# Four normalised residual layers on one core: the norms' inverse roots computed by Newton steps on GpSimd, and the sigmoid table loaded once

## The chip, the cores and the metric

The kernel runs on one core of a Trainium2 chip. The metric is the device time of one execution in microseconds (us), as the median of several runs. The engines of the core are called PE (TensorE, the matrix engine), DVE (VectorE), ACT (ScalarE) and POOL (GpSimd); SP (SyncE) issues most of the DMAs. Each engine carries out its own instructions in the order in which the program lists them, and waits for the others through semaphores.

## The reference

The input x has the shape 4 x 32 x 32 x 16. Four layers run one after the other, each as `x = x + L(_gn(x))`. The norm `_gn` forms, for each image and each group of two channels, the mean and the variance over all pixels of the group:

```python
m = jnp.mean(g, axis=(1, 2, 4), keepdims=True)
s = jnp.var(g, axis=(1, 2, 4), keepdims=True)
return ((g - m) / jnp.sqrt(s + eps)).reshape(v.shape)     # eps = 1e-5
```

Layers 0, 1 and 3 are convolutions whose 3x3 filters G differ at each of the 1024 output positions: `first` is a product of the positions with a 1024 x 1024 matrix M, and `second` is the sum over all pixels of W times `relu(input - shifted)`, where `shifted` is the image filtered with that position's filters. Layer 2 is an interval layer: running maxima and minima over a triangle, two steps of `max(sigmoid(ft + rt + b))`, and a last sigmoid.

## The kernel before, in words

The images are handled as two groups g of two. The three convolutions on two groups make six phases (`phases`, L90); a phase has 8 chunks of 128 output positions, a chunk 32 steps, so 256 steps a phase and 1536 in all. A step (L719) is one filter channel f of one image b. Each step lists, in this order:

- one resumption of the generator `prep_parts` (L220), which gets the filters of later steps ready;
- `first_part` of this step (L644): 8 matmuls into a pair of PSUM banks and an ACT pass over them (L665);
- `second_part` of the step before (L668): 6 more matmuls into its banks, and then one DVE instruction, called junk here (L682), which takes the minimum with zero, multiplies by W and sums. The pool of bank pairs has four buffers (L80), so the first product of a step needs that the junk four steps earlier is done;
- where its pause has run out, one resumption of the generator `behind` (L735), which carries everything else: norms, interval layer, the next phase's images, the products with M.

The engines are not in step with one another; a step only says where in each engine's list an instruction stands.

`prep_parts` gets one unit of filters (4 channels, used in 8 steps) ready in 8 resumptions, two units ahead of its use. With k for the resumption, 0 to 7: k=0 `upper` on DVE (L203, tile upper_w), which needs that POOL has centred this unit's raw filters; k=1 an ACT pass (L175); k=2 an ACT pass and on POOL the tensor operations of L237 and L238; k=3 an ACT pass and on POOL L241 and four casts (L243, L245); k=4 on POOL the centring of the raw filters of the NEXT unit (L214, tile raw); k=6 on SP two copies of the parts and the load of later raw filters (L251, L110). In phase 0 the resumptions begin at step 3 with two extra ones at steps 20 and 24, so that from step 24 on, and in every later phase, step s of a phase has k = (s - 1) mod 8. The tile upper_w has two buffers, parts has three.

`behind` says by the value that it yields how many steps it pauses. The value IDLE (0) means: go on at the next step whose resumption of `prep_parts` allows it (k = 0, 4, 5, 6, 7). So each pause in `behind` sets which k its next piece of work falls on, and what stands ahead of it on POOL, DVE, ACT and SP.

`group_norm` (L315) occurs eight times: c00 and c10 in phase 0, c01 in phase 1, c11 in phase 2, i0 and c02 in phase 3, i1 and c12 in phase 4 (the letter says convolution or interval layer, then for c the group and the convolution, for i the group). DVE reduces (`sums`, `totals`, L317 to L341), POOL centres and squares (L347 to L351), DVE reduces again and ends with the transpose `whole`; then ACT takes the root (L361), DVE the reciprocal (L363), and POOL multiplies (L364). Between `sums` of the squares and its `totals` stands a one-element Sqrt (L356), to have the table of Sqrt loaded in time, and in `step` of the interval layer a one-element Sigmoid (L593) ahead of the real one (L596). ACT has one set of tables active at a time; the compiler puts an ACT_TABLE_LOAD ahead of an activation whose function is not in it. The first Sqrt of the kernel is that of the opening (L834), which stays.

After i0 and i1, DVE transposes the normalised images in two pieces (L510), at two neighbouring steps. `split` and `difference` (L274, L286) put two more kinds of POOL operations (L280, L288) into the end of the work for a next phase, and `place` (L290) twelve DMAs for each image. `first_terms` (L420) multiplies both groups with M, 128 small matmuls in a row (L427).

Of the kernel before, what the change touches and what calls it, by code (L numbers as in the profile page):

```python
# [8 lines left out]
F32 = mybir.dt.float32  # L9
F32R = mybir.dt.float32r  # L10
I32 = mybir.dt.int32
AF = mybir.ActivationFunctionType
ALU = mybir.AluOpType
AX = mybir.AxisListType

P = 128
# [3 lines left out]
GC = GB * C  # L20
NL = 3
NP = H * H
# [22 lines left out]
def net_kernel(ctx: ExitStack, tc: tile.TileContext, x, xq, xi, convs, iv_w, iv_b, out):  # L45
# [26 lines left out]
    nc = tc.nc  # L72
# [4 lines left out]
    work = ctx.enter_context(tc.tile_pool(name="work", bufs=1))  # L77
# [5 lines left out]
    def bank_pair(name):  # L83
        return psum.tile([P, 2, 512], F32, tag="ps", name=name)
# [13 lines left out]
    IDLE = 0  # L98
# [55 lines left out]
    spare = const.tile([1, 1], F32, name="spare")  # L154
    nc.gpsimd.memset(spare, 0.0)
    eps = const.tile([P, 1], F32, name="eps")
# [152 lines left out]
    def spread(stat):  # L309
        return stat.unsqueeze(1).unsqueeze(3).to_broadcast([P, NT, GC // 2, 2])  # L310

    def pair_view(ap):
        return ap.rearrange("p t (g s) -> p t g s", s=2)

    def group_norm(g, name, dst, gap):  # L315


        def sums(src):
            nc.vector.tensor_reduce(
                part[:, : GC // 2], src.rearrange("p t (g s) -> p g t s", s=2), axis=AX.XY, op=ALU.add  # L320
            )

        def totals(name):

            turned = work.tile([P, 32], F32, tag="turned", name=f"turned_{name}")
            nc.vector.transpose(turned, part)
            by_quarter = work.tile([32, 4], F32, tag="by_quarter", name=f"by_quarter_{name}")
            for q in range(4):
                nc.vector.tensor_reduce(
                    by_quarter[:, q : q + 1], turned[32 * q : 32 * q + 32], axis=AX.X, op=ALU.add  # L330
                )
            yield gap
            total = work.tile([P, 32], F32, tag="total", name=f"total_{name}")
            for q in range(4):
                nc.vector.tensor_reduce(
                    total[32 * q : 32 * q + 32, 0:1], by_quarter, axis=AX.X, op=ALU.add
                )
            yield gap
            whole = work.tile([P, 32], F32, tag="whole", name=f"whole_{name}")
            nc.vector.transpose(whole, total[:, 0:1].to_broadcast([P, 32]))  # L340
            return whole[:, : GC // 2]  # L341

        sums(X[g])
        yield gap
        m = yield from totals(f"m{name}")
        mean = work.tile([P, GC // 2], F32, tag="mean", name=f"mean_{name}")
        nc.gpsimd.tensor_scalar_mul(mean, m, 1.0 / (2 * NP))  # L347
        xc = work.tile([P, NT, GC], F32, tag="xc", name=f"xc_{name}")
        nc.gpsimd.tensor_tensor(pair_view(xc), pair_view(X[g]), spread(mean), ALU.subtract)
        sq = work.tile([P, NT, GC], F32, tag="sq", name=f"sq_{name}")  # L350
        nc.gpsimd.tensor_tensor(sq, xc, xc, ALU.mult)  # L351
        yield 4
        sums(sq)
        yield gap
        yield IDLE
        nc.scalar.activation(spare, spare, AF.Sqrt)  # L356
        v = yield from totals(f"v{name}")
        yield 2
        yield IDLE
        rstd = work.tile([P, GC // 2], F32, tag="rstd", name=f"rstd_{name}")  # L360
        nc.scalar.activation(rstd, v, AF.Sqrt, bias=eps, scale=1.0 / (2 * NP))  # L361
        yield 2
        nc.vector.reciprocal(rstd, rstd)  # L363
        nc.gpsimd.tensor_tensor(pair_view(dst), pair_view(xc), spread(rstd), ALU.mult)  # L364
        yield 3

# [4 lines left out]
    def before_conv(g, layer):  # L371
        xn = work.tile([P, NT, GC], F32, tag="xn", bufs=2, name=f"xn_{g}_{layer}")
        xns[g] = xn
        yield from group_norm(g, f"c{g}{layer}", xn, 1 if layer == 2 else 4)


# [43 lines left out]
    def first_terms(layer, mt):  # L420


        sums = bank_pair(f"pf_{layer}")
        for g in range(NG):
            for pt in range(NT):
                for j in range(4):
                    nc.tensor.matmul(  # L427
                        sums[32 * j : 32 * j + 32, g, :256],
                        lhsT=xns[g][:, pt, :], rhs=mt[:, pt, j, :],
                        start=pt == 0, stop=pt == NT - 1, tile_position=(0, 32 * j),  # L430
                    )
        ft = work.tile([P, NG, NT * GC], F32, tag="fs", name=f"ft_{layer}")
        for g in range(NG):
            nc.vector.transpose(ft[:, g], sums[:, g, : NT * GC])
        yield 1
        for g in range(NG):
            nc.vector.tensor_tensor(
                X[g], X[g], ft[:, g].rearrange("p (t m) -> p t m", t=NT), ALU.add
            )
            yield 1  # L440
# [45 lines left out]
    def interval_layer(g):  # L486
# [4 lines left out]
        n = H * H  # L491
# [10 lines left out]
        nc.gpsimd.memset(r[:R, :, 0:1], 0.0)  # L502
        nc.gpsimd.memset(r[:R, H:], 0.0)
        yield from group_norm(g, f"i{g}", xi, 2)

        raw = one[:GC].rearrange("p (j t r) -> p r t j", j=H, r=ROWS)
# [65 lines left out]
        def step(name, ftp, bias):  # L572

            ft = ivp.tile([P, QI, T1], F32, tag="ft", name=f"ft_{name}{g}")
            nc.scalar.copy(ft, ftp)
            yield 2
            s = ivp.tile([P, QI, T1], F32, tag="s", name=f"s_{name}{g}")
            last = None
            for i in range(QI + 1):
                if i < QI:  # L580
                    t = dp[i % 2]
                    nc.gpsimd.tensor_tensor(
                        t,
                        ft[:, i, :].unsqueeze(1).to_broadcast([P, T1, T1]),
                        rt,
                        ALU.add,
                    )
                if last is not None:
                    nc.vector.tensor_reduce(s[:, i - 1, :], last, axis=AX.X, op=ALU.max)
                last = t  # L590
                yield 6 if i < QI else 3
            yield IDLE
            nc.scalar.activation(spare, spare, AF.Sigmoid)  # L593
            yield 2
            yield IDLE
            nc.scalar.activation(s, s, AF.Sigmoid, bias=bias)  # L596
            for q in range(NQ):
                nc.sync.dma_start(r[R:, QI * q : QI * (q + 1), :], s[GC * q : GC * (q + 1)])
            yield 4

        yield from right_side("r0", iv["r0"])
        ftp = left("l0", iv["f0"])
        yield from step("a", ftp, bv[:, 0:1])
        yield from right_side("r1", iv["r1"])
        ftp = left("l1", iv["f1"])
        yield from step("b", ftp, bv[:, 1:2])
        z = left("l2", iv["f2"])
        y = ivp.tile([P, QI, H], F32, tag="y", name=f"y_{g}")
        nc.scalar.activation(y, z[:, :, 1:], AF.Sigmoid, bias=bv[:, 2:3])
        yield 2  # L610
        y = y.rearrange("p i j -> p (i j)")
# [370 lines left out]
```

## Time and profile before

| | |
|---|---|
| three runs | 2480.47, 2481.87, 2485.29 us; median 2481.87 |
| the profiled execution, its own time | 2481.97 us |
| its span in the profile | 2480.3 us, granted clock 1.00 |
| PE busy | 2458.5 us, 99% |
| DVE busy | 2086.0 us, 84% |
| ACT busy | 1878.2 us, 76% |
| POOL busy | 1579.3 us, 64% |
| PE idle for ACT / for DVE's junk / for a parts DMA | 5.2 / 2.9 / 1.7 us in all |
| table loads | 5: one for L834, two for L356, two for L593, 1.283 us each |

A busy share is an average over the whole span. The PE row says how little can be won, because the other engines' time lies beside PE's. Which engine holds PE up, and where, is read from the view of waits and from the timeline of a stretch, where each line has the start, the length, the engine, the line of the code and the tiles.

### The profile page before, as it was taken

The page shows a single profiled execution, that of the slowest core. Times are in us where ns is not written, and L with a number is a line of the kernel's source. Part 1 is how long each engine was busy: PE and PEld are TensorE (multiplying, and loading weights), DVE is VectorE, ACT ScalarE, POOL GpSimd, SP SyncE. Part 2 cuts the span into 40 slices and gives each one's busy share as a digit, 9 for nine tenths or more (in the row PEclk, how much of TensorE's full clock was granted, in tenths as well). Part 3 has the DMA queues.
Part 4 walks back from the last instruction along what each step waited for, and adds up shares of the span by engine and source line. Part 5 has one row for each costly group of instructions (what it writes and reads, how often), then busy time and mean ns, then how long its engine had stood idle before and what let it go on. Part 6 is the DMA issues. An engine that isn't in the chain of part 4 may idle for free.

```text
span 2480.3 us, 58060 instructions
## 1 busy us (share of the span) xinstructions
PE 2458.5 (99%) x21906; PEld 2074.2 (84%) x21906; DVE 2086.0 (84%) x3617; ACT 1878.2 (76%) x2181; POOL 1579.3 (64%) x1750
## 2 busy tenths in 40 slices
PE   8999999999999999999999999999999999999999
PEld 4888888888888888888888989888989888888887
DVE  8888878888888888788898988899889888788887
ACT  3778767787777778677777777787777787677776
POOL 4766655667555667555567777586778676555552
PEclk9999999999999999999999999999999999999999
DMA  6556744465454457544454545574455477554442
GB/s 189 140 144 183 213 131 134 138 180 157 137 145 137 137 157 193 176 137 137 137 145 119 143 126 139 146 195 124 129 139 145 120 187 201 150 145 137 137 137 54
DMA packets 97673, 366.92 MB, mean 148 GB/s; under 512 B 26480, under 2 KB 31472, under 8 KB 97392
## 3 DMA queue, kind: packets, MB, share of 16 engines
q1 hardware_dynamic: 95696, 361.57, 52.9%
q8 instruction: 172, 2.82, 0.5%
q10 hardware_dynamic: 1568, 1.62, 0.3%
q14 instruction: 109, 0.89, 0.1%
q0 software_dynamic: 128, 0.02, 0.0%
HBM read 199.78 MB, written 1.02 MB: 81 GB/s over the span
## 4 chain that ended last, share of the span: by engine, by line
PE 94%; DVE 2%; DMA 2%; issue 1%; ACT 1%; POOL 0%; SPq 0%; ACTq 0%; DVEq 0%; POOLq 0%
PE pc L629 92%; DVE junk L682 1%; PE pf L427 1%; DMA parts<-parts 1%; ACT pc L665 0%; DMA raw<-in_xi 0%; DMA raw<-in_g 0%; DMA ia<-first 0%; PE ps_l L550 0%; DMA first<-in_g 0%; PE ps_r L563 0%; DVE tables L510 0%; DVE raw L848 0%; DVE upper_w L203 0%; SPq L302 0%
## 5 line engine op out<-in xcount | busy, mean ns | idle before, releaser
L682 DVE SCALAR_TENSOR_TENSOR junk<-pc,WT 128x1024 f32<-128x1024 f32 x1536 | 1880.0, 1224 | 363.6 <-PE pc L629 316.8
L665 ACT ACTIVATE pc<-pc 128x1024 f32<-128x1024 f32 x1520 | 1531.8, 1008 | 556.1 <-PE pc L629 531.6
L629 PE MATMUL pc<-ib,parts 64*128 64x512 f32 x6080 | 953.0, 387 | 4.7 <-DVE junk L682 2.9
L629 PE MATMUL pc<-iyz,parts 64*128 64x512 f32 x6080 | 950.3, 387 | 5.3 <-ACT pc L665 5.2
L629 PE MATMUL pc<-ia,parts 64*128 64x496 f32 x6080 | 928.5, 379 | 0.0
L629 PEld LDWEIGHTS pc<-ib,parts 64*128 64x128 f32 x6080 | 585.1, 184 | 109.3 <-DVE junk L682 8.5
L629 PEld LDWEIGHTS pc<-ia,parts 64*128 64x128 f32 x6080 | 587.6, 184 | 106.2
L629 PEld LDWEIGHTS pc<-iyz,parts 64*128 64x128 f32 x6080 | 586.2, 184 | 94.9 <-ACT pc L665 9.4
L629 PE MATMUL pc<-im,W 64*128 64x496 f32 x3072 | 606.4, 384 | 0.0
L237 POOL TENSOR_TENSOR parts<-raw,upper_w 128x512 fp32r<-128x512 f32 x190 | 249.0, 1311 | 496.3 <-DVE upper_w L203 447.3
L629 PEld LDWEIGHTS pc<-im,W 64*128 64x128 f32 x3072 | 297.8, 184 | 57.3 <-issue 3.6
L243 POOL CAST parts<-parts 32x512 fp32r<-32x512 f32 x380 | 231.2, 608 | 48.8 <-ACT parts L240 30.5
L238 POOL TENSOR_TENSOR W<-W,raw 128x512 fp32r<-128x512 f32 x190 | 246.9, 1300 | 7.8 <-ACT W L175 7.8
L241 POOL TENSOR_TENSOR parts<-parts 128x512 fp32r<-128x512 f32 x190 | 246.5, 1297 | 2.2 <-ACT parts L236 2.0
L245 POOL CAST parts<-upper_w 32x512 fp32r<-32x512 f32 x380 | 231.6, 609 | 22.8
L214 POOL TENSOR_TENSOR raw<-raw,ident 128x512 f32<-128x512 f32 x190 | 199.5, 1050 | 61.5 <-DMA raw<-in_g 36.6
L175 ACT ACTIVATE W<-raw,low_w 128x512 fp32r<-128x512 f32 x190 | 136.2, 717 | 9.2 <-DMA ia<-first 9.2
L682 DVE DVE_READ_ACCUMULATOR junk<-pc,WT 128x1 f32 x1536 | 127.8, 83 | 0.0
L236 ACT ACTIVATE parts<-upper_w 128x512 fp32r<-128x512 f32 x190 | 118.8, 625 | 4.8 <-DVE upper_w L203 4.7
L240 ACT CAST parts<-upper_w 128x512 fp32r<-128x512 f32 x190 | 116.6, 614 | 0.0
L697 POOL TENSOR_SCALAR acc<-acc 128x32 f32<-128x32 f32 x40 | 16.7, 417 | 136.5 <-DVE junk L682 134.6
L203 DVE TENSOR_SCALAR upper_w<-raw 128x512 int32<-128x512 int32 x190 | 85.2, 449 | 2.7 <-POOL raw L214 2.3
(139 smaller groups left out, 479.1 us busy)
## 6 DMA issues: line engine op xcount, KB each, us to landing
raw<-in_g SPq DMA_DIRECT2D x190, 768.0 KB, 7.1
parts<-parts SPq DMA_DIRECT2D x380, 384.0 KB, 5.0
WT<-in_w SPq DMA_DIRECT2D x48, 512.0 KB, 4.6
MT<-in_mt SPq DMA_DIRECT2D x24, 512.0 KB, 7.9
raw<-xs SPq DMA_DIRECT2D x120, 71.8 KB, 3.1
ib<-temp SPq DMA_DIRECT2D x40, 128.0 KB, 2.4
ia<-temp SPq DMA_DIRECT2D x80, 62.0 KB, 3.4
raw<-in_xi SPq DMA_DIRECT2D x3, 287.0 KB, 5.0
```

The costliest lines, as they stand in the source:

```text
L175: nc.scalar.activation(dst, src, AF.Copy, scale=mask[:, 1:2])
L214: eng.tensor_tensor(raws[u][:, s, at:to], raws[u][:, s, at:to], pick[s][:, f0 + at : f0 + to].unsqueeze(2).to_broadcast([P, to - at, P]), ...
L236: nc.scalar.activation(WD, high, AF.Copy, scale=-EPS)
L237: nc.gpsimd.tensor_tensor(WL, w8, high, ALU.subtract)
L238: nc.gpsimd.tensor_tensor(W9, W9.bitcast(F32), src[:, 2], ALU.add)
L240: nc.scalar.copy(WU, high)
L241: nc.gpsimd.tensor_tensor(WD, WD.bitcast(F32), WL.bitcast(F32), ALU.add)
L243: nc.gpsimd.tensor_copy(WU[hi], WL[lo].bitcast(F32))
L245: nc.gpsimd.tensor_copy(WL[lo], high[hi])
L629: nc.tensor.matmul(ps[:, h, at : at + n], lhsT=w[r], rhs=v[r] if n == NH else v[r][:, :n], start=first and k == 0, stop=k == len(pairs) - ...
L665: nc.scalar.activation(ps, ps, AF.Copy, scale=1.0 + EPS)
L682: nc.vector.scalar_tensor_tensor(junk, ps.rearrange("p h n -> p (h n)"), 0.0, chunks[n], op0=ALU.min, op1=ALU.mult, accum_out=accs[phase][ ...
```

## The change

A new generator `inverse_root` replaces the ACT root and the DVE reciprocal of a norm. POOL forms a = v/2048 + 1e-5; DVE forms a first guess y of the inverse root from a's bits with two integer operations (a shift, then a subtraction from a constant); POOL halves and negates a, and then makes four Newton steps of four operations each, y = y (1.5 + a y y), with a pause of one step behind each. All are on tiles of 128 x 16 elements. The one-element Sqrt ahead of it is taken out, and with it two IDLE pauses and two of two steps; a pause of one step comes in. In the interval layer, the one-element Sigmoid of `step` goes, with an IDLE pause and one of two steps. One one-element Sigmoid is put into `first_terms`, for the first convolution only, behind its matmuls in the program.

```diff
--- before.py
+++ after.py
@@ -312,6 +312,28 @@
     def pair_view(ap):
         return ap.rearrange("p t (g s) -> p t g s", s=2)
 
+    def inverse_root(v, name):
+
+        n = GC // 2
+        a, y, t = (
+            work.tile([P, n], F32, tag=tag, name=f"{tag}_{name}") for tag in ("root_a", "root_y", "root_t")
+        )
+        nc.gpsimd.tensor_scalar(a, v, 1.0 / (2 * NP), 1e-5, op0=ALU.mult, op1=ALU.add)
+        nc.vector.tensor_scalar(
+            t.bitcast(I32), a.bitcast(I32), 1, None, op0=ALU.logical_shift_right
+        )
+        nc.vector.tensor_scalar(
+            y.bitcast(I32), t.bitcast(I32), -1.0, float(0x5F3759DF), op0=ALU.mult, op1=ALU.add
+        )
+        nc.gpsimd.tensor_scalar_mul(a, a, -0.5)
+        for _ in range(4):
+            nc.gpsimd.tensor_tensor(t, a, y, ALU.mult)
+            nc.gpsimd.tensor_tensor(t, t, y, ALU.mult)
+            nc.gpsimd.tensor_scalar(t, t, 1.5, None, op0=ALU.add)
+            nc.gpsimd.tensor_tensor(y, y, t, ALU.mult)
+            yield 1
+        return y
+
     def group_norm(g, name, dst, gap):
 
 
@@ -352,15 +374,9 @@
         yield 4
         sums(sq)
         yield gap
-        yield IDLE
-        nc.scalar.activation(spare, spare, AF.Sqrt)
         v = yield from totals(f"v{name}")
-        yield 2
-        yield IDLE
-        rstd = work.tile([P, GC // 2], F32, tag="rstd", name=f"rstd_{name}")
-        nc.scalar.activation(rstd, v, AF.Sqrt, bias=eps, scale=1.0 / (2 * NP))
-        yield 2
-        nc.vector.reciprocal(rstd, rstd)
+        yield 1
+        rstd = yield from inverse_root(v, name)
         nc.gpsimd.tensor_tensor(pair_view(dst), pair_view(xc), spread(rstd), ALU.mult)
         yield 3
 
@@ -429,6 +445,8 @@
                         lhsT=xns[g][:, pt, :], rhs=mt[:, pt, j, :],
                         start=pt == 0, stop=pt == NT - 1, tile_position=(0, 32 * j),
                     )
+        if layer == 0:
+            nc.scalar.activation(spare, spare, AF.Sigmoid)
         ft = work.tile([P, NG, NT * GC], F32, tag="fs", name=f"ft_{layer}")
         for g in range(NG):
             nc.vector.transpose(ft[:, g], sums[:, g, : NT * GC])
@@ -589,9 +607,6 @@
                     nc.vector.tensor_reduce(s[:, i - 1, :], last, axis=AX.X, op=ALU.max)
                 last = t
                 yield 6 if i < QI else 3
-            yield IDLE
-            nc.scalar.activation(spare, spare, AF.Sigmoid)
-            yield 2
             yield IDLE
             nc.scalar.activation(s, s, AF.Sigmoid, bias=bias)
             for q in range(NQ):
```

## The prediction, made before the changed kernel was run

> **What bounds the kernel now.** I read the page first, then PE's waits, then the timelines around a table load and around the norm i0. The page says that PE is full:
>
> ```profile
> PE 2458.5 (99%) x21906; PEld 2074.2 (84%) x21906; DVE 2086.0 (84%) x3617; ACT 1878.2 (76%) x2181; POOL 1579.3 (64%) x1750
> ```
>
> No PE work is added or removed, so the change can only alter the 21.8 us in which PE is idle (2480.3 - 2458.5). PE's waits, with total, number and longest:
>
> ```profile
> PE pc L629 <- ACT pc L665: 5.2, 7, 1.6
> ...
> PE pc L629 <- DVE junk L682: 2.9, 8, 0.8
> ```
>
> Of the 5.2 us on ACT, 3.2 us lie before 60 us and 0.4 us at the very end; the four others are one gap of 0.38 to 0.39 us at each of the four table loads of L593 and L356. The first of these on ACT (start, length):
>
> ```profile
> 1423.04 1.01 ACT L665 ACTIVATE pc<-pc 128x1024 f32<-128x1024 f32 x1 [0.56 <-PE pc L629]
> 1424.06 1.28 ACT L593 ACT_TABLE_LOAD   x1
> 1425.36 0.20 ACT L593 ACTIVATE spare<-spare 1x1 f32<-1x1 f32 x1
> 1425.47 1.89 ACT L665 ACTIVATE pc<-pc 128x1024 f32<-128x1024 f32 x2
> ```
>
> ACT idles 0.56 us per step, and a step lasts 1.567 us (the pitch of the waiting junks): most of the load is absorbed. Now POOL and DVE around i0:
>
> ```profile
> 1273.91 1.30 POOL L237 TENSOR_TENSOR parts<-raw,upper_w 128x512 fp32r<-128x512 f32 x1 [5.46 <-DVE upper_w L203]
> 1275.16 1.30 POOL L238 TENSOR_TENSOR W<-W,raw 128x512 fp32r<-128x512 f32 x1
> 1276.41 1.31 POOL L241 TENSOR_TENSOR parts<-parts 128x512 fp32r<-128x512 f32 x1
> 1277.79 1.27 POOL L243 CAST parts<-parts 32x512 fp32r<-32x512 f32 x2
> 1279.12 1.27 POOL L245 CAST parts<-upper_w 32x512 fp32r<-32x512 f32 x2
> 1280.48 1.04 POOL L214 TENSOR_TENSOR raw<-raw,ident 128x512 f32<-128x512 f32 x1
> ```
>
> ```profile
> 1284.83 0.42 DVE L203 TENSOR_SCALAR upper_w<-raw 128x512 int32<-128x512 int32 x1
> ...
> 1287.96 1.31 DVE L510 STREAM_TRANSPOSE tables<-xi 32x256 f32<-32x256 f32 x2
> 1289.31 1.23 DVE L682 SCALAR_TENSOR_TENSOR junk<-pc,WT 128x1024 f32<-128x1024 f32 x1
> ...
> 1290.57 1.30 DVE L510 STREAM_TRANSPOSE tables<-xi 32x256 f32<-32x256 f32 x2
> 1291.90 1.23 DVE L682 SCALAR_TENSOR_TENSOR junk<-pc,WT 128x1024 f32<-128x1024 f32 x1
> ```
>
> The reader is to see a loop: `upper` on DVE starts POOL's unit, and POOL's last operation of the unit (L214, done at 1281.52) is what the next `upper` reads. That one comes at 1284.83, so POOL has 3.3 us in hand, once a unit. DVE's own slack follows from the two transposes: the junk at 1291.90 is 1.95 us behind the pitch, and PE waited 0.21 us there, so DVE may fall some 1.74 us behind before PE stops.
>
> **What the Trainium skill says.** "ScalarE: Activation LUTs", What ACT_TABLE_LOAD costs: about 1283 ns and a drain of 1380 ns for a switch of sets. The trace agrees on the load (1.283 us); of the drain it shows nothing behind the load, as the next activation starts 0.02 us after its end. The same page, Table sets: cheap functions such as copy are in every set; the trace agrees, since L665 runs under either set without a load. "GPSIMD Engine Reference", Instruction dispatch: consecutive Pool instructions don't order the cores, so a dependent one must wait for the producer's semaphore. That applies to every Newton operation; in the trace a dependent POOL operation starts 0.08 us after its producer's end (L697 to L698), an independent one 0.05 us before it (L237 to L238). "Trainium Architecture — The Big Picture", What this means for kernel authors: VectorE and GpSimd share a port pair under an exclusive lock. The trace agrees: beside POOL's L280 at 1633.21, an `upper` took 1.43 us against a median of 0.42.
>
> **The change, part by part.**
>
> *Table loads.* Four of five go; built, the changed ScalarE list holds one for L834 and one in `first_terms`. Removed from PE's path: 4 x 0.385 = 1.5 us. The new load (1.28 + 0.20 us) stands beside the 128 products with M, which keep PE busy for 7.04 us while ACT has no pc to pass over: nothing. Without that cover it would cost 0.4 us like the others. The eight Sqrt (0.30 us) fit ACT's idle 0.56 us and go for nothing, as do the one-element activations.
>
> *DVE.* A reciprocal (0.25 us) is replaced by two integer operations; the nearest row is TENSOR_SCALAR 128x16 at 0.17 us, so +0.1 us a norm, inside the slack. But the shift waits for POOL's a, and the next junk stands behind it. With k = (s - 1) mod 8, the pauses put it on k=1 for c00 (step 42), i0 and i1 (step 18), on k=4 for c01 and c11 (step 29), on k=6 for c10 (87), c02 and c12 (191). Only at k=4 is POOL in the way: in phase 1, L214 ends 8.16 us after the unit's `upper` and the junk ahead of the shift at 7.80. With a (0.25 us) and two semaphores DVE waits some 0.8 us, under 1.74: nothing.
>
> *POOL.* Per norm 2 + 16 operations. TENSOR_SCALAR 128x16 has a row: 0.25 us (L347). TENSOR_TENSOR 128x16 has none: 128x32 takes 0.25, 64x32 0.23; I take 0.22. With 0.08 us between dependents a Newton step is 3 x 0.30 + 0.33 = 1.23 us. Bounds: 0.85 us, if they follow one another at 0.21 us like the four of L461 (0.83 us); 1.75 us, if each costs the 0.42 us mean of L697.
>
> Where it is queued decides. At k=1, POOL's list is: a, the halving (which waits for DVE's shift), Newton step 1, L237, L238, step 2, L241 and casts, step 3, L214, step 4, multiplication. In i0: DVE is through with the junk ahead of the shift at 1276.36; shift to 1276.53; 0.13 us to POOL (as from `upper` to L237); halving to 1276.91; step 1 from 1276.98 to 1278.15. So L237 starts at 1278.2 instead of 1273.91, 4.3 us late, although its input was there. Steps 2 and 3 add 2.46 us ahead of the end of L214: 1281.52 + 4.3 + 2.46 = 1288.3. The next `upper` stands ready at 1284.83 and waits 3.5 us, with the junks behind it on DVE, and PE behind those. The transposes now follow at once (pauses: the same step as that `upper` and the next), with no step between to recover. DVE's list from 1288.4: upper 0.42, junk 1.31, transposes 1.31 (from 1290.4, when xi is there), junk 1.31, transposes 1.31; the junk after that starts at 1294.4, where the pitch gives 1288.38. That is 6.0 us, less the slack of 1.74: PE idles 4.3 us, 4.0 more than the 0.21 now (rounding aside). i1 has the same timeline 412 us later: 4.0 again.
>
> c00: the junk ahead of its shift ends at 90.4 once the sums in front of it are a step earlier; POOL's halving to 90.97, step 1 to 92.2, L237 at 92.25 instead of 87.88, 4.37 us late; L214 ends at 95.48 + 4.37 + 2.46 = 102.3. `upper` is due at 99.66 and waits 2.77 us with the semaphore; with the 0.09 us by which it exceeds DVE's idle 0.33, 2.86 - 1.74 = 1.1 us. No transposes follow.
>
> At k=4 the Newton steps fall into POOL's free part and push the next L237 by about 1.5 us; at k=6 they start at 11.6 us of the unit, end at 16.85, and push the next L237 by 3.7 us. Its L214 then ends, with the norm's 0.68 us multiplication, about 25.0 us after the first `upper`, and the DVE's turn is at 25.1: nothing, but close.
>
> *Moved.* `behind` runs earlier: by 8 steps at the end of phase 0, 16 in phases 3 and 4, none in 1 and 2. With it move the loads of M, the copies of xs, and `place` on SP, and `split` and `difference` on POOL, past the parts copies. The two other gaps that come from such neighbours (1.7 us for a parts DMA at 273.6, 0.8 us at 1638) may go or come again elsewhere: zero, with 2 us either way. Late parts: at k=1 their casts end 5.5 us later (4.3 + 1.23); PE needs them 15 steps or 23.5 us after `upper`, and now they end 7.0 us after it, which with the page's 5.0 us to landing leaves some 11 us. Covered.
>
> *Sum*, on the profiled execution: 2481.97 - 1.5 + 4.0 + 4.0 + 1.1 = 2489.6. It took 0.1 us more than the median of the runs shown, so 2489.5 (+0.31%).
>
> **The rivals.**
>
> *Main case, 0.58.* PE waits for junk behind a late `upper` at i0, i1, c00. With Newton steps of 0.85 us, each site's L214 ends 1.15 us earlier: 2.85 at i0 and i1, 0 at c00: +5.7 - 1.5 = +4.2, 2486. With 1.75 us, 1.56 later: 5.6 + 5.6 + 2.7 - 1.5 = +12.4, 2494. Its own range is 2485 to 2494.
>
> *Not slower: the loop's slack holds, 0.24.* POOL idles 447 us for `upper` in all, and `upper` waited for L214 only 2.3 us. If POOL fits the Newton steps into that idle time so that L214 ends before 1284.83 + 1.74 = 1286.6 at i0, only the loads count: 2480.4. It decides at a lateness of 5.0 us against the 6.8 that I count. The order in the list speaks against it: 2.46 us stand ahead of L214 and cannot overtake it.
>
> *Worse, 0.12.* The lock between POOL and DVE lengthens `upper` or the Newton operations on top, as at 1633, or late casts send a parts DMA into PE's path (as at 273.6, 1.7 us): main case plus 2 to 6 us, about 2493.
>
> *The loads come back, 0.03.* An activation elsewhere could need Sqrt again; the built list shows none. 2491.0.
>
> *Faster by more than 0.2%, 0.03.* It needs 5 us; the loads hold 1.5 and all of PE's waits after the opening 5.5.
>
> **How the numbers follow.** 0.2%, about what a measurement of this kernel can tell from no change, is 5.0 us: 2476.9 to 2486.8. Slower: main 0.52 of 0.58, worse 0.12, loads back 0.02: 0.66. Same: 0.24 and the lower end of the main case, 0.06, and 0.01: 0.31. Faster: 0.03. The range reaches from the case in which the slack holds, 2480, to the dear Newton steps with something on top, 2495.
>
> **What would show it.** In the profile after: PE's wait for DVE junk of about 12 us instead of 2.9, nearly all at three places, near 100, 1290 and 1705 us; DVE's wait of `upper` for POOL's raw of about 10 us instead of 2.3; L237 4.3 us late at those sites; TENSOR_TENSOR 128x16 at 0.22 us; two table loads, and PE's wait for ACT of 3.7 us. I am wrong if `upper` doesn't wait at i0, or if PE idles elsewhere, at the k=4 or k=6 norms or for a parts DMA.

## The result, and the profile after

The changed kernel takes 2503.83 us (median of five runs, 2502.16 to 2507.88) beside 2480.47 us for the kernel before on the same chip (five runs, 2478.81 to 2485.29). The ratio is 1.0091, with a 95% interval from 1.0080 to 1.0101. The forecast was slower, 2489.5 us, with a range up to 2495: the sign is right, the time lies 8.8 us above the range. The profiled execution has a span of 2501.8 us against 2480.3, 21.5 us more.

The line of the page that was read first before, now of the kernel after:

```profile
PE 2467.7 (99%) x21906; PEld 2092.4 (84%) x21906; DVE 2088.2 (83%) x3625; ACT 1872.2 (75%) x2159; POOL 1611.9 (64%) x1894
```

PE has the same 21906 matmuls but is busy 9.2 us longer (2467.7 - 2458.5), so its idle time accounts for only 12.3 of the 21.5 us. PE's waits in the kernel after (total, number, longest):

```profile
PE pc L644 <- DVE junk L697: 10.4, 14, 1.1
PE pc L644 <- DMA parts<-parts: 7.0, 6, 1.4
PE pc L644 <- ACT pc L680: 4.7, 4, 1.9
```

The first line answers to the 2.9 us of before and is near the 12 us forecast, but by luck in part: only 5.4 of the 10.4 us (gaps at 103, 1291 to 1297 and 1711 to 1717) stand at the three places forecast. The second is new in size. It was, in the kernel before:

```profile
PE pc L629 <- DMA parts<-parts: 1.7, 1, 1.7
```

For the place, I took the ends of the junk of the same step in both traces; the kernel after falls behind by the growth of their difference over a stretch. It grows by 1.95 us in phase 0, 0.1 in phases 1 and 2, 2.9 at i0, 7.0 from about step 200 of phase 3 to its end, 2.9 at i1 and 9.6 from about step 200 of phase 4. In between it falls by 1.4 and 1.6, where two table loads each are gone (0.77 us of each; the rest isn't assigned). Sum: 1.95 + 0.1 + 2.9 - 1.4 + 7.0 + 2.9 - 1.6 + 9.6 = 21.5.

**At i0.** POOL's timeline of the kernel after (start, length, engine, line, tiles, and in brackets the idle time before it), cut to what stands ahead of L214:

```profile
1278.06 0.25 POOL L328 TENSOR_SCALAR root_a_i<-root_a_i 128x16 f32<-128x16 f32 x1 [1.12 <-DVE root_t_i L322]
1278.40 0.22 POOL L330 TENSOR_TENSOR root_t_i<-root_a_i,root_y_i 128x16 f32<-128x16 f32 x1
...
1279.53 1.29 POOL L237 TENSOR_TENSOR parts<-raw,upper_w 128x512 fp32r<-128x512 f32 x1
...
1287.20 0.22 POOL L330 TENSOR_TENSOR root_t_i<-root_a_i,root_y_i 128x16 f32<-128x16 f32 x1
...
1288.33 1.04 POOL L214 TENSOR_TENSOR raw<-raw,ident 128x512 f32<-128x512 f32 x1
```

and DVE's at the same place:

```profile
1289.40 0.43 DVE L203 TENSOR_SCALAR upper_w<-raw 128x512 int32<-128x512 int32 x1 [2.46 <-POOL raw L214]
...
1291.33 1.31 DVE L528 STREAM_TRANSPOSE tables<-xi 32x256 f32<-32x256 f32 x2 [0.36 <-POOL xi L380]
...
1293.94 1.30 DVE L528 STREAM_TRANSPOSE tables<-xi 32x256 f32<-32x256 f32 x2
```

This is the loop as predicted: three of the four Newton steps (here the first and the third are shown) stand ahead of L214, 1.13 us each from their first start to the next operation (1278.40 to 1279.53), and `upper` waits 2.46 us behind L214. The two transposes follow at once.

**At the end of phase 3** (the norm c02 and the next phase's images; c12 at the end of phase 4 is the same). SP's queue in the kernel after:

```profile
1576.77 16.23 SPq L411 DMA_DIRECT2D raw<-xs  x24
1593.16 1.10 SPq L251 DMA_DIRECT2D parts<-parts  x2
```

and in the kernel before:

```profile
1591.68 5.64 SPq L395 DMA_DIRECT2D raw<-xs  x12
1597.48 1.11 SPq L251 DMA_DIRECT2D parts<-parts  x2
...
1599.95 9.96 SPq L395 DMA_DIRECT2D raw<-xs  x12
```

The 24 loads of the shifted images stood around the k=6 copies, twelve ahead and twelve behind. The pauses that are gone, most of them in the interval layer (the squares of c02 already stand 11 steps earlier), move them from steps 212 to 217 (k = 3 to 0) to steps 200 to 205 (k = 7 to 4), where all 24 fall between two k=6 copies. SP issues them in one block of 16.23 us, though six steps last only 9.4 us. Not all of the block is the work of issuing: SP's own waits in it, from 1576 to 1593 us, are one line, 2.5 us in which the eighth load waits until the raw filters issued at 1575.46 have landed:

```profile
SPq L411 <- DMA raw<-in_g: 2.5, 1, 2.5
```

What is held up shows on POOL in the kernel after:

```profile
1580.34 1.28 POOL L245 CAST parts<-upper_w 32x512 fp32r<-32x512 f32 x2
...
1603.72 1.04 POOL L214 TENSOR_TENSOR raw<-raw,ident 128x512 f32<-128x512 f32 x1 [10.50 <-DMA raw<-in_g]
```

The first casts end at 1581.62 and their copies are issued at 1593.16, 11.5 us later. From there they take 3.8 and 5.1 us to land, which is usual (5.0 is the median), so what made these two late is the issue and not the transfer. The raw filters, issued behind them at 1594.37, land so late that POOL waits 10.5 us. PE then stops twice for copies (1.42 and 1.34 us), once for ACT (0.86) and once for junk (1.09). PE's busy time and granted clock (PEclk) there, in two neighbouring stretches behind those gaps of the kernel after:

```profile
1607.90:1611.30 3.40, 3.40 (x18) 2.71 (x18) 3.40 (x4) 1.41 (x2) 3.40 (x3) 0.51 0.79 183
1611.30:1615.00 3.70, 3.70 (x36) 3.08 (x36) 3.43 (x8) 3.13 (x5) 3.64 (x4) 1.00 0.41 96
```

Columns: the stretch, its length, busy time of PE, PEld, DVE, ACT, POOL with counts, PEclk, DMA share, GB/s. PE runs 3.4 us at a clock of 0.51 and starts 18 matmuls in place of the some 33 that the next stretch would give in that time (36 in 3.70 us). Such stretches make up most of PE's longer busy time: the kernel after has 3.4 us from 48.0, 3.4 from 1607.9 and 6.8 from 2027.7 us, the kernel before none ahead of its last 3 us. Half of 13.7 us is 6.8 of the 9.2 us; the other 2.4 us aren't assigned.

### The profile page after: what moved, and what is told of

It is laid out like the page before. It is cut to its first block, busy times and chain, and to the rows that moved or that the text cites. A ratio compares the mean times of both kernels' runs of the same rounds, so it can differ in the third digit from the quotient of the medians.

```text
span 2501.8 us, 58178 instructions
## 1 busy us (share of the span) xinstructions
PE 2467.7 (99%) x21906; PEld 2092.4 (84%) x21906; DVE 2088.2 (83%) x3625; ACT 1872.2 (75%) x2159; POOL 1611.9 (64%) x1894
## 4 chain that ended last, share of the span: by engine, by line
PE 88%; DVE 3%; DMA 3%; POOL 3%; issue 2%; SPq 1%; ACT 0%; ACTq 0%; DVEq 0%; POOLq 0%
PE pc L644 87%; DVE junk L697 3%; DMA raw<-in_g 2%; PE pf L443 1%; DMA parts<-parts 1%; SPq L411 0%; POOL parts L241 0%; POOL parts L245 0%; POOL parts L243 0%; POOL raw L214 0%; ACT pc L680 0%; POOL parts L237 0%; DMA first<-in_g 0%; DMA raw<-xs 0%; POOL iyz L288 0%
## 5 line engine op out<-in xcount | busy, mean ns | idle before, releaser
L644 PE MATMUL pc<-ib,parts 64*128 64x512 f32 x6080 | 965.3, 389 | 17.3 <-DVE junk L697 10.4
L644 PE MATMUL pc<-ia,parts 64*128 64x496 f32 x6080 | 938.3, 380 | 0.0
L644 PEld LDWEIGHTS pc<-ib,parts 64*128 64x128 f32 x6080 | 593.8, 185 | 123.3 <-DVE junk L697 18.6
L644 PEld LDWEIGHTS pc<-ia,parts 64*128 64x128 f32 x6080 | 598.3, 185 | 101.9
L644 PEld LDWEIGHTS pc<-iyz,parts 64*128 64x128 f32 x6080 | 594.9, 185 | 91.2 <-ACT pc L680 8.4
L644 PE MATMUL pc<-im,W 64*128 64x496 f32 x3072 | 614.4, 385 | 0.0
L237 POOL TENSOR_TENSOR parts<-raw,upper_w 128x512 fp32r<-128x512 f32 x190 | 249.0, 1310 | 465.8 <-DVE upper_w L203 409.1
L644 PEld LDWEIGHTS pc<-im,W 64*128 64x128 f32 x3072 | 305.1, 185 | 55.2 <-issue 3.3
L214 POOL TENSOR_TENSOR raw<-raw,ident 128x512 f32<-128x512 f32 x190 | 199.5, 1050 | 93.5 <-DMA raw<-in_g 77.3
L238 POOL TENSOR_TENSOR W<-W,raw 128x512 fp32r<-128x512 f32 x190 | 247.6, 1303 | 8.3 <-ACT W L175 8.3
L241 POOL TENSOR_TENSOR parts<-parts 128x512 fp32r<-128x512 f32 x190 | 246.9, 1299 | 2.1 <-ACT parts L236 2.1
L203 DVE TENSOR_SCALAR upper_w<-raw 128x512 int32<-128x512 int32 x190 | 88.2, 464 | 24.0 <-POOL raw L214 23.7
```

Of the source, the lines that this page charges most:

```text
L214: eng.tensor_tensor(raws[u][:, s, at:to], raws[u][:, s, at:to], pick[s][:, f0 + at : f0 + to].unsqueeze(2).to_broadcast([P, to - at, P]), ...
L237: nc.gpsimd.tensor_tensor(WL, w8, high, ALU.subtract)
L238: nc.gpsimd.tensor_tensor(W9, W9.bitcast(F32), src[:, 2], ALU.add)
L241: nc.gpsimd.tensor_tensor(WD, WD.bitcast(F32), WL.bitcast(F32), ALU.add)
L644: nc.tensor.matmul(ps[:, h, at : at + n], lhsT=w[r], rhs=v[r] if n == NH else v[r][:, :n], start=first and k == 0, stop=k == len(pairs) - ...
```

## The experiments

The theory after the result: (a) the Newton steps delay L214 at i0 and i1, 2.9 us each; (b) the larger loss is the shifted image work, with its 24 loads in one block. The rival to (b): the Newton steps make POOL late there too. Ratios are to the kernel before on the same chip; its medians lie from 2480.47 to 2483.34 over the chips, so ratios are compared and not times. Line numbers shift by a few in kernels with added lines.

**pause4: four steps more behind the norm in layer 2.**

```diff
         yield from group_norm(g, f"c{g}{layer}", xn, 1 if layer == 2 else 4)
+        if layer == 2:
+            yield 4
```

> The changed kernel with a pause of 4 more steps between the norm and the copies of xs in the layer behind the interval layers (c02, c12), and nothing else. The 24 loads raw<-xs then stand at k = 3 to 0, with the k=6 parts copies between the first 12 and the last 12, as in the kernel before; in the changed kernel all 24 stand between two k=6 places. Queue theory: the 24 loads in one block on SP hold up the parts copies and the next raw filters; apart, the 17 us that phases 3 and 4 lose there go: 2503.8 - 17 = about 2487 us, PE's wait for parts DMAs at 1595 and 2016 us gone. Rival, Newton lateness: POOL's Newton steps make xn late and everything behind it; they are unchanged, so the loss stays for the most part: 2498 us or more.

Measured 2492.59 us (2490.79 to 2496.84), ratio 1.0044 [1.0032, 1.0057]. About half of the loss goes (1.0091 to 1.0044), without one operation less. SP's queue in this kernel is again as before:

```profile
1583.44 5.86 SPq L413 DMA_DIRECT2D raw<-xs  x12
1589.46 1.87 SPq L251 DMA_DIRECT2D parts<-parts  x2
...
1592.62 9.25 SPq L413 DMA_DIRECT2D raw<-xs  x12
```

**no_newton: the four operations of each Newton step left out, the pauses kept.** Left out is the refinement of the inverse root; the first guess is used.

```diff
         for _ in range(4):
-            nc.gpsimd.tensor_tensor(t, a, y, ALU.mult)
-            nc.gpsimd.tensor_tensor(t, t, y, ALU.mult)
-            nc.gpsimd.tensor_scalar(t, t, 1.5, None, op0=ALU.add)
-            nc.gpsimd.tensor_tensor(y, y, t, ALU.mult)
             yield 1
```

> The changed kernel with the sixteen Newton operations of each norm left out and all pauses kept: y is the first guess from the bits, so the norms are some per cent off. Queue theory: the loads stay between two k=6 places, so most of the 17 us at c02 and c12 stay; only PE's waits behind a late upper at i0, i1 and c00 go (about 6 us): 2498 us. Rival, Newton lateness: both losses come from POOL's Newton work and go together: 2480 to 2483 us.

Measured 2500.46 us (2497.8 to 2502.35), ratio 1.0072 [1.0060, 1.0085]. PE's wait for the copies in this kernel:

```profile
PE pc L640 <- DMA parts<-parts: 7.6, 6, 1.7
```

The waits for the copies are all there without a Newton step. The rival falls. At i0 and i1 the loss is gone (0 and 0.07 us); at c02 and c12 it stays (7.8 and 8.9 us).

**root_k4: the root begins at k=4.** `inverse_root` starts in POOL's free time behind L214; the copies and loads are left in their block.

```diff
         v = yield from totals(f"v{name}")
-        yield 1
+        yield IDLE
         rstd = yield from inverse_root(v, name)
```

> The changed kernel with the pause of one step ahead of the root replaced by an IDLE pause: at c00, i0 and i1 the root moves from k=1 to k=4, behind POOL's L214; at the five other norms nothing moves, and the work of c02 and c12 stands at the same steps. Theory of the late upper: Newton steps ahead of L214 make upper wait at i0 and i1, 2.5 us each, and cost 5.5 us with what follows; here that goes: 2498 us, upper's wait for POOL at 1289 us gone. Rival: the stall is of the transposes that follow upper at once; they still follow xi, so some 2 us at each site would stay: 2501.5 us.

Measured 2495.0 us (2492.72 to 2497.64), ratio 1.0052 [1.0039, 1.0064]. The loss at i0 and i1 falls to 0.09 and 0.07 us, that at c02 and c12 stays (8.2 and 10.6 us in its profile). The gain is larger than the 5.8 us of i0 and i1; the rest lies in phase 0, see below.

**pause4_k4: both edits.**

> Both edits: the pause of 4 steps ahead of the copies of xs for c02 and c12, and the root behind an IDLE pause. If the two losses are apart and each edit takes one away, the sum is 2503.8 - 17 - 5.5 = 2481 us, level with the kernel before (2480.5). If a third loss is behind both, it stays over 2486 us.

Measured 2482.59 us (2480.2 to 2486.48, 13 runs), ratio 1.0003 [0.9995, 1.0011]. The two edits add up: 0.0047 and 0.0039 of the 0.0091 apart, 0.0088 together. PE waits once for the copies in this kernel, 0.6 us.

**What inside the shifted work costs.** Six kernels tried to separate the loads, the copies and the image work.

*loads_only*: pause4, but the pause behind the loads is cut from 6 to 2, so that `split` and `place` come early and the loads stand as before.

```diff
-        yield 6 if layer == 2 else 12
+        yield 2 if layer == 2 else 12
```

> The changed kernel with the copies of xs and the 24 loads raw<-xs of c02 and c12 four steps later, as in pause4, but with the pause behind the loads cut from 6 to 2 steps, so that split, place and difference stay at the steps of the changed kernel. It tells apart the two things that pause4 moved. Queue theory: what counts is that a k=6 place falls between the loads; the gain of pause4 (11 us) comes back for the most part: 2493 to 2496 us, less if DVE now meets the loads too early and waits for them. Rival, POOL's split and difference at the wrong k delay L214: they are unmoved, so nothing is gained: 2502 us or more.

Measured 2510.0 us, ratio 1.0111 [1.0097, 1.0125], slower than either theory had it. It tells nothing on the question, since DVE now met the loads before they had landed, as DVE's waits in this kernel show:

```profile
DVE upper_x L203 <- DMA raw<-xs: 19.4, 2, 10.4
```

*image_later*: the opposite, all else as in the kernel after; the pause behind the loads in layer 2 goes from 6 to 14.

> The changed kernel with the pause behind the loads raw<-xs of c02 and c12 lengthened from 6 to 14 steps: split, place and difference come 8 steps later, the loads stay in one block where they were. If the loss is SP's queue alone (copies and raw filters behind 24 loads), it stays for the most part: 2498 us or more. If it is the loads and the image work close together (loads late for split, raw filters late, place behind them on SP, all within two units), it goes for the most part: 2487 to 2491 us.

Measured 2500.91 us (2496.88 to 2504.3), ratio 1.0071 [1.0059, 1.0083]. The loss at c02 and c12 is 5.9 us each in the profiled execution, the slowest of the five: most of it needs no `place` behind the loads.

*parts_by_act*: in the two bad stretches, ACT's queue issues the copies of parts (u is the unit).

```diff
+            eng = nc.scalar if u in (123, 124, 155, 156) else nc.sync
             for h in range(2):
-                nc.sync.dma_start(
+                eng.dma_start(
```

> The changed kernel with the parts copies of two units in each of phases 3 and 4 (those whose k=6 stands at or behind the loads raw<-xs, steps 207 and 215) issued by ACT instead of SP; every pause as it was, the raw filters still on SP. Queue theory: the copies no longer stand behind 24 loads, so PE's waits for parts DMAs near 1595 and 2016 us (5.4 us in all, and the slower clock behind them) go; the raw filters still come late, so upper's wait and its part of the loss stay: about 2494 us. Rival, the transfers themselves compete with one another or POOL is late: 2502 us or more.

Measured 2500.15 us, ratio 1.0072 [1.0060, 1.0085]. *both_by_act* moves the load of raw filters that follows (L110) too:

> As parts_by_act, with the loads of the raw filters of the same two units also issued by ACT. Queue theory: nothing that PE needs soon is behind the 24 loads now; both kinds of wait go at c02 and c12, with the Newton steps, the pauses and all places unchanged: 2503.8 - 17 = 2487 us. Rival, the places of the work on POOL and DVE or the load on the DMA engines: it stays over 2498 us.

Measured 2501.01 us, ratio 1.0079 [1.0066, 1.0093]. Both are near the rival's number, but not for its reason. ACT's timeline in both_by_act shows that ACT stood at the copies:

```profile
1584.96 1.19 ACTq L252 DMA_DIRECT2D parts<-parts  x2
...
1587.50 1.93 ACT L681 ACTIVATE pc<-pc 128x1024 f32<-128x1024 f32 x2 [5.59 <-issue]
```

ACT does no pass between 1581.9 and 1587.5 and PE gets a gap of 4.6 us from that (3.4 us in parts_by_act). The trace tells what ACT waited for until 1584.9. In these kernels the DMAs of SP and ACT take eight semaphores in turn, and each waits until the DMA that had its semaphore before has landed. ACT's first copy got that of the raw filters which SP had issued at 1575.80; they landed at 1584.86, and the copy was issued at 1584.96. So the move to ACT didn't free the copies, and it stopped ACT. *both_by_pool* is the same with POOL's queue:

> As both_by_act, with POOL issuing the parts copies and the raw filters of the two units. POOL makes the parts itself, so it waits for nothing at that place, and its queue has semaphores of its own; in both_by_act ACT stood still for 4.6 us at the copies and PE behind it, which hid what the test was for. Price: three issues of about 0.6 us a unit on POOL (as its xs<-zero takes now). Queue theory: 2487 us and some, up to 2491. If the loss stays over 2498 us, it isn't that the copies and filters stand behind the loads on SP.

Measured 2499.85 us (2493.64 to 2504.18), ratio 1.0064 [1.0052, 1.0076]. By the mark set beforehand this is against the theory in its narrow form, that only the copies and filters behind the loads cost. The profile, of the fastest of six executions, shows what came instead. The waits for copies are gone (0.6 us in all), and the next thing in SP's block comes out: in DVE's timeline of both_by_pool, `split` waits for the loads themselves, and PE loses 3.5 and 4.1 us in two gaps.

```profile
1592.66 0.74 DVE L203 TENSOR_SCALAR upper_x<-raw 128x1024 int32<-128x1024 int32 x1 [4.83 <-DMA raw<-xs]
```

*loads_on_two_queues*: all pauses, copies and raw filters as in the kernel after; POOL's queue issues every second of layer 2's loads.

```diff
-                nc.sync.dma_start(
+                (nc.gpsimd if layer == 2 and h else nc.sync).dma_start(
                     raw[r0 : r0 + C, slot ^ h if slot < 2 else 2, :, :RUN], xsv[:, h, :, off : off + RUN]
                 )
```

> The changed kernel with every pause as it is; in layer 2 half of the 24 loads of xs (the ones with h = 1) are issued by POOL's queue and not by SP's, so that SP's block of issues is about 8 us long and not 16, and POOL issues 12 DMAs more at about 0.6 us each. If the length of SP's block is what holds the copies of parts and the raw filters behind it, the 16.6 us lost in phases 3 and 4 shrink to a half or less: 2494 to 2497. Rival, that the transfers themselves or the semaphores that they share hold them: the loss stays, 2501 or more; POOL's issues, some 7 us in each of the two stretches, can hide a part of the gain.

Measured 2492.51 us (2490.71 to 2499.71), ratio 1.0047 [1.0034, 1.0059]. SP's queue in this kernel:

```profile
1575.55 11.80 SPq L411 DMA_DIRECT2D raw<-xs  x12
1587.52 1.22 SPq L251 DMA_DIRECT2D parts<-parts  x2
```

The block is 11.80 us instead of 16.23. I had expected 8, but SP waits 4.5 us in it for DMAs to land, 3.3 of them for raw filters. The copies are issued 1.7 us after their casts (at 1585.8) instead of 11.5, PE waits 0.9 us for copies in all instead of 7.0, and the loss at c02 and c12 falls from 7.0 and 9.6 to 2.5 and 4.2 us. The DMA engines are no less busy for it (DMA share 0.90 from 1575 to 1588 us and 1.04 from 1588 to 1594), which speaks against a rival by which the transfers crowd one another out. With not one step of `behind` moved, nearly half of the loss goes (1.0091 to 1.0047). The edit brings the copies, the raw filters and the loads forward together; what each of them costs alone, no run here shows.

**spread_k4: the block spread out.** root_k4, and one pause behind every row of loads, so that the 24 loads are listed two a step over 12 steps.

```diff
-            if layer < 2 or row % 2:
-                yield 1
+            yield 1
```

> A version meant to beat both: the root behind an IDLE pause (as root_k4), and the loads raw<-xs of c02 and c12 at two a step over 12 steps, as in the other layers, instead of four a step over 6. Queue theory: SP has time for the copies between the loads, so what phases 3 and 4 still lose in pause4_k4 (0.7 and 4.2 us) goes too, and the table loads are saved: 2482.6 - 4 = about 2478 us. If the loss there is of the loads' number and not of their crowding, it stays at 2482 us or more.

Measured 2478.04 us (2475.68 to 2480.5, 21 runs), ratio 0.9978 [0.9972, 0.9985]: faster than both kernels. PE's waits in this kernel:

```profile
PE pc L643 <- DVE junk L696: 3.0, 7, 1.1
...
PE pc L643 <- DMA parts<-parts: 0.9, 1, 0.9
```

The wait for junk is down from 10.4 us to 3.0 and that for the copies from 7.0 to 0.9. All Newton operations are in it (POOL has the same 1894 instructions), and PE's busy time is 2457.3 us, back to that of before. The edit also puts `split` and `place` six to eight steps later; image_later, which does that alone by eight, stood at 1.0071.

**spread_k4_loads: the price of a table load.** spread_k4 with two one-element Sqrt ahead of the roots of c02 and c12 and a one-element Sigmoid in each interval step put back.

> spread_k4 with three table loads put back, at the kernel before's places in the interval layer and at c02 and c12, with no pause changed (the fourth has no switch to make, since the first Sigmoid of phase 3 has its table already). Each should cost PE the 0.38 us that it cost before: 1.2 us over spread_k4, 2479.2 us, and three gaps of 0.4 us behind ACT in the profile. If a load costs its whole 1.28 us or drains more, 4 us or over.

Measured 2479.35 us (2477.62 to 2483.4, 21 runs), ratio 0.9988 [0.9982, 0.9995]. The ratios of the two differ by 0.0010 (2.5 us), and their intervals overlap, so the times don't tell 1.2 us from 4. The trace does for PE: it has a gap of 0.38 or 0.39 us at each of three loads that came back, 1.2 us. A gap of 1.98 us at 1647, which spread_k4 lacks, stands behind a late load of raw filters (ACT waits 2.38 us for it) and at none of the table loads.

**old_pauses and pauses_mended: the changed operations at the pauses of before.** old_pauses puts back the IDLE and two-step pauses of the norm and of the interval step, and cuts the norm's last pause from 3 to 1 to keep its length (the two pauses of the interval step are left out below).

```diff
         yield gap
+        yield IDLE
         v = yield from totals(f"v{name}")
-        yield 1
+        yield 2
+        yield IDLE
         rstd = yield from inverse_root(v, name)
         nc.gpsimd.tensor_tensor(pair_view(dst), pair_view(xc), spread(rstd), ALU.mult)
-        yield 3
+        yield 1
```

> The changed kernel with the pauses of the kernel before: IDLE ahead of the sums of the squares, two steps and IDLE ahead of the root, the two pauses in the interval layer's step, and the pause behind the norm cut by two so that the Newton steps' four steps fit. Everything outside the root stands at the steps of the kernel before; the operations are those of the change. The root falls on k=7 in phase 0 and on k=4 elsewhere. If the pauses, that is the places, are the whole loss: the loads saved and nothing lost, 1.5 us under the kernel before, about 2480 us on this chip. If the operations themselves (Newton on POOL, two more on DVE) carry part of it: over 2486 us.

Measured 2507.22 us (2505.45 to 2508.82), ratio 1.0097 [1.0083, 1.0112]: a plain miss. c02 and c12 lose little (1.1 and 2.0 us), i0 and i1 0.9 each, but three gaps of 4.34 us are new, near 186, 503 and 912 us, at c10, c01 and c11, each with 6.8 us at half clock behind it. DVE's timeline at the first:

```profile
188.96 0.45 DVE L396 STREAM_TRANSPOSE xt<-xn 128x256 f32<-128x256 f32 x1 [5.55 <-POOL xn L382]
```

My edit had put the transpose one step behind POOL's last multiplication. pauses_mended keeps the three steps in layers 0 and 1 and takes two from the pause behind the loads (12 becomes 10).

> The changed operations with the kernel before's pauses, as in the last try with them, but the three steps between the norm's last multiplication and DVE's transpose of it are kept in layers 0 and 1 and taken out of the pause behind the loads (12 becomes 10). Theory, that the change costs only by where its pauses put the other work: the three gaps of 4.3 us in the middle of phases 0 to 2, each with a stretch at half clock, were the transpose put one step behind POOL's multiplication; they go, and the whole stands at 2480 to 2484 beside 2482.5 of before. Rival, that the new operations hold the engines by themselves: the gaps stay or move, 2490 or more.

Measured 2491.93 us (2486.02 to 2494.64), ratio 1.0036 [1.0024, 1.0048]. The theory's number missed again, the rival's is met. c02 and c12 lose 1.5 and 1.0 us, i0 and i1 0.8 each. The three gaps are still there with 1.2 us each. POOL's timeline at the first:

```profile
184.21 0.23 POOL L330 TENSOR_TENSOR root_t_c<-root_a_c,root_y_c 128x16 f32<-128x16 f32 x1
...
188.03 1.28 POOL L245 CAST parts<-upper_w 32x512 fp32r<-32x512 f32 x2
189.39 0.67 POOL L382 TENSOR_TENSOR xn<-xc_c,root_y_c 128x256 f32<-128x256 f32 x1
```

In phases 0 to 2 the old pauses put the root's start on k=7, so that its last Newton step falls behind L237 and L238, and its multiplication behind L241 and the casts; DVE's transpose of xn waits 2.8 us for it. So the theory that only the moved work costs is wrong in that form: the new operations cost by their place, nothing seen at k=4 in phases 1 and 2 of the kernel after, 2.9 us a norm at k=1, and a gap of 1.2 us at k=7 here.

## Why the prediction was wrong in its size

The sign was right, and one mechanism of it; the size was wrong by one step.

- *"Moved ... zero, with 2 us either way"*, and within it *"Late parts ... Covered"*: this is the step that failed. The text names the copies of xs and `place` on SP and says that they move past the parts copies, but prices neither. It leaves the 24 loads of raw from xs out of its list. And it gives one length for the move in phases 3 and 4, 16 steps. That is two whole units, which leave every k as it was, and it holds for the end of the work (the second `place`, step 239 to 223); the copies of xs and the 24 loads move by 12 (212 to 200), from k = 3 to 0 to k = 7 to 4 (in phases 1 and 2 it is one step, where I had none). The stretch cost 7.0 + 9.6 = 16.6 us. I had asked only how late POOL's casts would be, and found some 11 us in hand at k=1; the copies were late by 11.5 us in SP's queue, at other units. In the trace of before, the two blocks of twelve loads (5.64 and 9.96 us) and the copies between them could be read; steps 200 to 205 follow from the pauses. pause4, which moves the steps, loads_on_two_queues, which moves the issues alone, and spread_k4 agree on it.
- *No price for PE's clock.* The sum counts gaps at their length. PE's busy time grew by 9.2 us, 6.8 of them because a bunch of gaps brings a stretch at half clock. At c02, gaps of 5.35 us (1.42 + 1.34 + 0.86 + 1.09 + 0.24 + 0.40) and 3.4 us at half clock (half of it lost) make 7.05; less the 0.79 us of gap that the kernel before has there, that is 6.3 of the 7.0 measured.
- *i0 and i1, 4.0 us each*: mechanism right, 2.9 each, 2.3 of them new gaps of PE (0.71 + 1.05 + 0.71 less the 0.21 of before, at i0). L237 was to be 4.3 us late and was 3.6 (1279.53 against 1273.91, less the 2.0 us by which the kernel was behind already). The halving was done at 1278.31 and L237 began at 1279.53, 1.22 us apart, where I had 1.3; `upper` waited 2.46 us instead of 3.5. root_k4 and no_newton both take it to nil.
- *c00, 1.1 us*: one gap of 0.38 us for it, at 103. The rest of phase 0 isn't told apart (below).
- *Newton operations*: 0.22 us for 128x16 was right, and so were the 0.08 us between dependents.
- *k=4 and k=6, nothing*: right at k=4 (no gap at c01 and c11, phases 1 and 2 grow by 0.1 us). At k=6, c02's and c12's Newton steps are not what costs there.
- *Table loads, -1.5 us*: the four gaps of 0.385 us are gone and no new one stands at the new load; spread_k4_loads brings three back at that price. PE's wait for ACT came to 4.7 us where I had 3.7, since gaps of 0.86 and 1.54 us behind the blocks are new.
- *DVE's operations and its wait for POOL's a, nothing*: right for PE. DVE waits twice for it, 1.2 us at most where I had 0.8, and PE has no gap there.
- *What would make it wrong*: "if PE idles elsewhere ... or for a parts DMA". That came, 7.0 us. The wait of `upper` for POOL's raw was to be about 10 us and is 23.7, with the late raw filters in it. Of the rivals, "Worse" had this cause, at 2 to 6 us on top and with late casts or the lock behind it, not SP's queue. Its time, 2493, is 10.8 us short.

Open: in phase 0, kernels with the same code there differ between -1.8 and +6.9 us against before in one profiled execution each, so the 1.95 us of the kernel after, and the 2.3 to 1.0 us that root_k4, pause4_k4, spread_k4 and spread_k4_loads gain there, aren't assigned. The four kernels at the upper end (3.7 to 6.9 us: parts_by_act, loads_only, no_newton, image_later) are those whose trace has a stretch at half clock near 266 us, behind waits for copies; the others have none there. Of the 2.5 and 4.2 us that stay in loads_on_two_queues, the trace shows `upper` waiting 3.5 us for L214 at c02, behind POOL's own new issues; what they would be without those wasn't tried.

## What to carry to other kernels

When a step gets shorter, everything listed after it moves: write down for each DMA behind it which queue it is on, how long the queue needs for its block, its own waits included, and which urgent copy now stands behind that block. Count the move for each of them apart: a whole number of periods changes nothing in its place, a part of one does. Price a cluster of stalls at more than the sum of its gaps where the granted clock falls afterwards. An operation that costs little by itself is free or dear by its place in the list: here the same 18 POOL operations cost 2.9 us a norm ahead of L214 and nothing behind it (0.1 in root_k4), and with the root there and the loads spread the change as a whole gains 0.22%.

## What the hardware showed that I had not expected

- A few gaps of about 1 us, none of them long, halved PE's clock: 0.86 + 1.09 us of idle within the 3.4 us up to 1607.9 were followed by 3.4 us at 0.51. The stretches at half clock in these traces are 3.4 or 6.8 us long, one 10.2, and their edges keep a grid of 3.413 us within each trace. Laid on that grid, the traces of all runs have 24 windows at full clock in which PE idled for over 54%: all 24 were followed by half clock. Of some 11500 under 43% none was, and of the 27 between 6 were. The Trainium skill, "TensorE: Matmul & The Clock Gate", What's actually happening, gives a free-running window of 3413 ns and a fall to half the clock after an idle window. The trace agrees on the lengths; the window at 1607.9 was not idle but 57% idle (1.95 of 3.4 us), so on that the measurement decides: about half was enough.
- The Trainium skill, "Perfetto Trace Analysis", What "DMA-bound" means, lists an issuing engine's sequencer that is solid with DMAs as a bound of its own. The trace agrees in part: SP spent 16.23 us on 24 small loads, and an urgent copy waited for the end of them. Most issues took 0.42 us, three 1.2 to 1.5 us, and 2.5 us were SP's own wait. Twelve took 5.64, 5.86, 9.25, 9.96 and 11.80 us in different places, so a count of DMAs alone doesn't give the time.
- Here a DMA that landed late stopped its queue eight DMAs on. The raw filters issued at 1575.46 landed at 1584.33, and the eighth DMA behind them on SP was issued at 1584.34; from 1581.85 to then SP issued nothing, and by the trace that DMA waited for nothing but their semaphore. The kernel before has the same: raw filters landed at 1607.73, and the eighth DMA behind them was issued at 1607.74. In both_by_act the raw filters' semaphore came to ACT's copy, and ACT stood in the same way.
- Of the four copies issued into that stretch, from 1593 to 1597 us in the kernel after, the two that PE waited for landed in the usual time (3.8 and 5.1 us, against a median of 5.0 over the whole run), and the two behind them late, after 9.5 and 10.6 us; the DMA share is 0.87 to 0.99 there.
- `upper` took 1.41 us at 1604.79, beside POOL's L280, against a median of 0.42: DVE's operation is slower beside POOL's here, as it was in the kernel before.
